# A four-layer graph network: first keys ahead of the branch, 125-row transfers on GpSimd, and the last block scanned in three parts

## The chip, the cores and the metric

The kernel runs on 1 core of one Trainium2 chip. The metric is the device time of one execution in microseconds (us). Engines: PE (TensorE) multiplies matrices, DVE (VectorE) works on vectors, ACT (ScalarE) evaluates functions, POOL (GpSimd) issues the indirect gathers and scatters here, SP (SyncE) issues most plain transfers.

## What is computed

There are N = 6250 nodes with D = 16 features and E = 200000 edges, sorted by their target `dst`. Each layer reads the source node's row for every edge, makes a message, combines the messages of each target, adds the node's own row and normalizes:

```
L0: m = tanh(x[src] * edge_weight);  x = layernorm(x + segment_sum(m, dst))
L1: attention over the edges (messages and weights from 16 edge features,
    softmax over each target's edges);  x = layernorm(x + ...)
L2: m = x[src] * edge_weight1;  x = layernorm(x + segment_max(m, dst) @ W.T + b)
L3: twice  h = relu(((1+eps)*h + segment_sum(h[src], dst)) @ wa + ba) @ wb + bb
    x = layernorm(x + log_softmax(h))
```

## The kernel before

**Layout.** Nodes lie on P = 125 partitions, NJ = 50 to each; edges on the same 125 partitions, J = 1600 consecutive ones to each. "Column" means one edge of each partition.

**Start.** SP loads dst, src and x. ACT's first instruction (`arrived`, L218) reads one element of src; behind it ACT's queue issues three copies from DRAM to DRAM (L220): `ew_d` and `ew1_d` (781 KB each) and `ef_d` (the edge features, 12.5 MB). DVE counts partitions whose dst isn't sorted (L225 to L230); every engine loads that number and branches (L231, L232): in the true branch `sort_edges` runs; with these inputs it is not taken. Behind the branch the keys of block 0 are made (`keys_made`, `keys_turned`, `keys_kept`, L246 to L280): DVE arithmetic on src, one transpose on PE, kT stored to `key_d` in DRAM (L274).

**edge_scan (L465)** runs four times: for L0, L2 and the two convolutions of L3 (l3a, l3b). The 1600 columns go in NB = 8 blocks of JB = 200. Of each block, the first NPE = 120 columns are fetched by PE: a batch of BC = 12 columns loads its keys (L456, SP, 367 KB, two batches ahead), DVE compares them with four node groups (`one_hot`, L462), and three `select`s of 4 columns each multiply one-hot matrices with the node table in SBUF (L491, 48 matmuls), after which DVE masks and reduces (L495, L500) into `xb`. The other 80 columns of the block are fetched by POOL, one indirect gather per column (L532, L97), of GP = 125 rows. Once a block is complete, DVE (and in L0 ACT) makes the message (`message`, L890/L891 in L0, L1292 in L2, nothing in L3), and 16 `tensor_tensor_scan`s, one for each feature, run along its 200 columns, beginning from the block before (L508 to L522). For blocks 0 to 6 this happens between the selects of the next block, two scans after each select; for block 7 it happens after the last select (L554 to L558). The running values are stored to `rows` in DRAM, and a short chain through PE carries totals between partitions (L560 to L584). The order of instructions in edge_scan is that of the program (`manual_schedule`).

**Side jobs.** In L0 the selects are numbered 0 to 239, and `prelude` (L893) hangs work onto them: keys of later blocks, the search for each node's last edge (`ends_*`), with 51 indirect run loads of 128 rows on POOL (`ends_gather`, L406), the chunk tables of L1, with 50 indirect scatters of 128 rows on POOL (`chunks_put`, L744), and the splitting of ef_d into `edges_d` (`edge_rows`). The edge weights `ew` of L0 are loaded on SP ahead of the scan (L887).

**at_nodes (L587)** follows each scan: 50 indirect gathers of 128 rows (`an_y`) fetch each node's last running value, in chunks `CHUNKS = ((0, 40), (40, 50))`; then `finish` makes the new node rows, stores them to the next table in DRAM (`into_table`) and splits them for PE. Its instructions are ordered by the scheduler, by estimates of cost.

**L1** runs 220 steps and then gathers its results, 50 indirect gathers of 128 rows into `r`, in groups of GN = 5 with 3 buffers; each group takes a Ln and an Exp on ACT, which load their function tables, and products and sums on DVE (L1224 to L1243).

Of the kernel before, what the change touches and what calls it, by code (L numbers as in the profile page):

```python
# [20 lines left out]
P = 125  # L21
# [20 lines left out]
CHUNKS = ((0, 40), (40, NJ))  # L42
# [5 lines left out]
def tile_gnn_resnorm(ctx: ExitStack, tc: tile.TileContext, a: dict, out: bass.AP):  # L48
# [166 lines left out]
    arrived = consts.tile([1, 1], F32, name="arrived")  # L215
    with tc.manual_schedule():

        nc.scalar.copy(arrived, src[:1, :1])  # L218
        for to, of in given[2:]:
            nc.scalar.dma_start(to.rearrange("(p j) f -> p (j f)", p=80),  # L220
                                of.rearrange("(p j) f -> p (j f)", p=80))
    with tc.tile_pool(name="sort", bufs=1) as sp, tc.tile_pool(name="sortp", bufs=1, space=PSUM) as pp:
        back = sp.tile([P, J], F32, name="backwards")
        worst = sp.tile([P, 1], F32, name="worst")
        nc.vector.tensor_tensor(back, dst[:, 1:J + 1], dst[:, :J], op=OP.is_lt)  # L225
        nc.vector.tensor_reduce(worst, back, AX.X, OP.max)
        n_ps = pp.tile([1, 1], F32, name="n_ps")
        nc.tensor.matmul(n_ps, worst, ones, start=True, stop=True)
        n_back = sp.tile([1, 1], I32, name="n_back")
        nc.vector.tensor_copy(n_back, n_ps)  # L230
        unordered = nc.values_load(n_back, min_val=0, max_val=P)  # L231
        with tc.If(unordered > 0):  # L232
            sort_edges(sp, pp, dst)
            nc.sync.dma_start(src, src_d.rearrange("(p j) o -> p (j o)", j=J))
            load_dst(dst, dst_d.rearrange("e o -> (e o)"))

# [42 lines left out]
    with tc.tile_pool(name="keys0p", bufs=1, space=PSUM) as pp:  # L279
        keys_kept(kp, 0, keys_turned(lambda r, c: pp.tile([128, 512], F32, name="scratch")[:r, :c], keys_made(kp, 0)))  # L280
# [74 lines left out]
    def ends_begin(sp):  # L355
        e = Ends()
        e.runs = sp.tile([P, NR + 1], F32, name="runs")
        nc.vector.tensor_copy(e.runs[:, :NR], dst[:, 1:J + 1].rearrange("p (r k) -> p r k", k=RUN)[:, :, RUN - 1])
        nc.vector.tensor_copy(e.runs[:, NR:], rank[:P])
        edge = sp.tile([P, 2], F32, name="dst_edge")  # L360
        nc.vector.tensor_copy(edge[:, 0:1], dst[:, :1])
        nc.vector.tensor_scalar(edge[:, 1:2], rank[:P], float(P - 1), BIG, op0=OP.is_equal, op1=OP.mult)
        nc.vector.tensor_add(edge[:, 1:2], edge[:, 1:2], e.runs[:, NR - 1:NR])

        e.from_ = sp.tile([P, 2, NJ1], F32, name="from_edge")
        nc.vector.tensor_tensor(e.from_, edge.unsqueeze(2).to_broadcast([P, 2, NJ1]),
                                io[:P, :NJ1].unsqueeze(1).to_broadcast([P, 2, NJ1]), op=OP.subtract)
        nc.vector.tensor_scalar(e.from_, e.from_, 1.0, None, op0=OP.add)
        e.run = sp.tile([P, NJ1], F32, name="run")
        e.run_i = sp.tile([128, NJ1], I32, name="run_i")  # L370
        nc.vector.memset(e.run_i[96:], 0)
        e.inside, e.row_ps = {}, {}
        return e
# [18 lines left out]
    def ends_runs(sp, e, j0):  # L392

        n = min(NS, NJ1 - j0)
        here = slice(j0, j0 + n)
        row_of = sp.tile([P, NS, NR + 1], F32, name="row_of")
        nc.vector.tensor_copy(row_of[:, :n], e.row_ps.pop(j0)[:, :n])
        less = sp.tile([P, NS, NR], F32, name="less")
        nc.vector.tensor_tensor(less[:, :n], row_of[:, :n, :NR], nodes[:, here].unsqueeze(2).to_broadcast([P, n, NR]),
                                op=OP.is_le)  # L400
        nc.vector.tensor_reduce(e.run[:, here], less[:, :n], AX.X, OP.add)
        nc.vector.scalar_tensor_tensor(e.run[:, here], row_of[:, :n, NR], float(NR), e.run[:, here], op0=OP.mult, op1=OP.add)
        nc.vector.tensor_scalar(e.run[:, here], e.run[:, here], float(E // RUN - 1), None, op0=OP.min)
        nc.vector.tensor_copy(e.run_i[:P, here], e.run[:, here])

    def ends_gather(sp, e):  # L406
        e.in_run = sp.tile([128, NJ1, RUN], I32, name="in_run")
        for j in range(NJ1):
            gather(e.in_run[:, j, :], runs_d, e.run_i[:, j:j + 1])

    def ends_upto(sp, e, j0):
        here = slice(j0, j0 + 17)
        less = sp.tile([P, 17, RUN], BF16, name="less_in")
        nc.vector.tensor_tensor(less, e.in_run[:P, here], nodes[:, here].unsqueeze(2).to_broadcast([P, 17, RUN]),
# [39 lines left out]
    def load_keys(ep, k, bufs=2):  # L454
        keys = ep.tile([P, BW], U16, name="keys", bufs=bufs)
        nc.sync.dma_start(keys, key_d[k * BC * P:k * BC * P + BW].partition_broadcast(P))  # L456
        return keys

# [6 lines left out]
    def edge_scan(tag, table, parts, F, message, pen, tmp, beside=None, first=None):  # L465
# [10 lines left out]
        with tc.tile_pool(name=f"es_{tag}", bufs=3) as ep, \  # L476
# [4 lines left out]
            NBT = NPE // BC  # L481
            batches = [(b, c) for b in range(NB) for c in range(NBT)]
# [19 lines left out]
            def scans(xb, b, prev):  # L502
# [3 lines left out]
                if prev is not None:  # L506
                    last = ep.tile([P, F], F32, name="last", bufs=2)
                    nc.vector.tensor_copy(last, prev[:, JB - 1, :])  # L508

                def one(f):  # L510
                    if is_max:
                        init = -BIG if last is None else last[:, f:f + 1]
                        nc.vector.tensor_tensor_scan(sc[:, :, f], pen[:, b * JB:(b + 1) * JB], xb[:, :, f],
                                                     init, op0=OP.add, op1=OP.max)
                    else:
                        init = 0.0 if last is None else last[:, f:f + 1]
                        nc.vector.tensor_tensor_scan(sc[:, :, f], keep[:, b * JB:(b + 1) * JB], xb[:, :, f],  # L517
                                                     init, op0=OP.mult, op1=OP.add)

                pieces = [lambda f=f: one(f) for f in range(F)]  # L520
                pieces.append(lambda: store(nc.sync, rows_v[:, b * JB:(b + 1) * JB, :], sc))
                return sc, pieces  # L522

            keys = [load_keys(ep, k) for k in range(0 if first is None else 1, 2)]
            ohs = one_hot(ep, keys.pop(0)) if first is None else first
            prev, todo, waiting = None, [], []
            for k, (b, c) in enumerate(batches):
# [10 lines left out]
                if c == 2 and waiting:  # L538
                    xw, bw = waiting.pop(0)
                    message(xw, bw)  # L540
                    prev, todo = scans(xw, bw, prev)
# [12 lines left out]
            for xw, bw in waiting:  # L554
                message(xw, bw)
                prev, todo = scans(xw, bw, prev)
                while todo:
                    todo.pop(0)()  # L558
# [150 lines left out]
    def chunks_set(tmp, num, stop, off_ps, all_ps):  # L709
# [16 lines left out]
        rows_all = tmp.tile([128, NJ, 4], F32, name="ck_rows")  # L726
        nc.vector.memset(rows_all[96:], 0.0)
        rows = rows_all[:P]
# [7 lines left out]
        at = tmp.tile([128, NJ], I32, name="ck_at")  # L736
        nc.vector.memset(at[96:], 128 * Q)
        nc.vector.tensor_copy(at[:P], first)
# [3 lines left out]
        return rows_all, at  # L742

    def chunks_put(rows_all, at):  # L744
        for j in range(NJ):
            nc.gpsimd.indirect_dma_start(
                out=chunk_d[j % NC], out_offset=bass.IndirectOffsetOnAxis(ap=at[:, j:j + 1], axis=0),
                in_=rows_all[:, j, :], in_offset=None, bounds_check=128 * Q - 1, oob_is_err=False)
# [138 lines left out]
    nc.sync.dma_start(ew, ew_d.rearrange("(p j) o -> p (j o)", j=J))  # L887

    def tanh_message(xb, b):
        nc.vector.tensor_mul(xb, xb, ew[:, b * JB:(b + 1) * JB].unsqueeze(2).to_broadcast([P, JB, D]))  # L890
        nc.scalar.activation(xb, xb, AF.Tanh)  # L891

    def prelude(kp):  # L893
# [65 lines left out]
        at(10, lambda: put(r=edge_rows_begin(now["rp"])))  # L959
        for i in range(J // WE):  # L960
            for step in range(4):
                at(16 + 3 * i + step, lambda i=i, step=step: edge_rows(now["r"], i * WE, step))
# [6 lines left out]
    rows, carry = edge_scan("l0", a["x"], parts, D, tanh_message, None, lp0, prelude(kp))  # L969
# [170 lines left out]
    first = one_hot(fp, load_keys(fp, 0, 1), 1)  # L1140
# [4 lines left out]
    with tc.tile_pool(name="l1t", bufs=1) as lp, tc.tile_pool(name="l1tp", bufs=1, space=PSUM) as pp:  # L1145
# [78 lines left out]
        for j0, j1 in CHUNKS:  # L1224
            n = j1 - j0
            y = lp.tile([P, n, D], F32, name=f"y1_{j0}")
            for j in range(j0, j1, GN):
                r = lp.tile([128, GN, RW], F32, name="r", bufs=3)
                for i in range(GN):
                    gather(r[:, i, :], rows1, idx_row_all[:, j + i:j + i + 1])  # L1230
                v = r[:P, :, :2 * DD].rearrange("p j (i k o) -> p j i k o", k=2, o=D)
# [3 lines left out]
                for i in range(GN):  # L1235
                    nc.vector.tensor_mul(A[:, i], A[:, i], L[:, i])
                    nc.vector.tensor_reduce(y[:, j - j0 + i, :], A[:, i].rearrange("p i o -> p o i"), AX.X, OP.add)
            nc.vector.tensor_mul(y, y, own[:, j0:j1].unsqueeze(2).to_broadcast([P, n, D]))
# [46 lines left out]
    with tc.tile_pool(name="l2", bufs=1) as lp:  # L1285
# [5 lines left out]
        def scaled_message(xb, b):  # L1291
            nc.vector.tensor_mul(xb, xb, ew1[:, b * JB:(b + 1) * JB].unsqueeze(2).to_broadcast([P, JB, D]))  # L1292

        rows, carry = edge_scan("l2", t2, parts, D, scaled_message, pen, lp, first=first)
        with tc.tile_pool(name="l2p", bufs=2, space=PSUM) as pp:
# [9 lines left out]
            at_nodes(lp, rows, carry, D, True, finish)  # L1305


    def gin(tag, table, parts, xt, F, ws, lp, then):
# [3 lines left out]
        rows, carried = edge_scan(tag, table, parts, F, lambda xb, b: None, None, lp, first=first)  # L1312
        with tc.tile_pool(name=f"{tag}p", bufs=2, space=PSUM) as pp:
# [21 lines left out]
            at_nodes(lp, rows, carried, F, False, finish)  # L1335
# [75 lines left out]
```

## Time and profile before

| what | us |
|---|---|
| median of 4 runs (7629.24 to 7634.75) | 7631.42 |
| the profiled execution | 7627.16 |
| its span, first to last instruction | 7625.4 |
| start, to the first matmul of L0 | 75.5 |
| L0 scan, POOL's first to last gather | 60.1 to 1220.2 |
| L0 running values done | 1238.4 |
| first gather of L1's steps' table | 1322.7 |
| L1's last step stored; end of its result gathers | 4217.9; 4297.8 |
| L2 gathers of xb | 4323.0 to 5333.1 |
| l3a gathers of xb | 5437.7 to 6432.0 |
| l3b gathers of xb | 6529.4 to 7522.0 |
| last store of out | 7622.4 |

| engine | busy us | share of the span |
|---|---|---|
| PE | 6790.1 | 89% |
| DVE | 6752.1 | 89% |
| POOL | 5864.3 | 77% |
| ACT | 1904.3 | 25% |

How to read it: the times of one profiled execution are counted from its first instruction; 1.8 us of the execution lie outside the span. A POOL row is the time in which POOL issues a gather, not that of the data's way. "idle before <- X" names what an engine waited for just before an instruction; "issue" is idle time without a recorded cause. L numbers are lines of the kernel before. In a row, `125x3200` is partitions x elements, and x16 stands for 16 instructions shown as one.

### The profile page before, as it was taken

Reading aid. Unit: us, or ns where it says so; the run is one execution under the profiler, and the core shown is the slowest. Engines: PE = TensorE matmul, PEld = TensorE weight load, DVE = VectorE, ACT = ScalarE, POOL = GpSimd, SP = SyncE. Lnnn points to the kernel's source line nnn. Section 1 sums busy time; section 2 is a strip of 40 time slices with the busy share of each in tenths; the row PEclk is TensorE's granted clock in tenths of the full one; section 3 lists DMA queues with packets and bytes.
Section 4 is the critical chain, followed back from the end, with each engine's and each line's share of the span. In section 5 each row is a group of like instructions: output and inputs, shape, how many; then the busy total and the mean of one; then the engine's idle time right before and its main releaser. Section 6 shows DMA issues by size and latency. Waiting matters only on the chain. (4 is left out here: it accounts for less than half of the span.)

```text
span 7625.4 us, 133196 instructions
## 1 busy us (share of the span) xinstructions
PE 6790.1 (89%) x55586; PEld 5218.0 (68%) x55586; DVE 6752.1 (89%) x7804; ACT 1904.3 (25%) x3200; POOL 5864.3 (77%) x4906
## 2 busy tenths in 40 slices
PE   5889894999999999999999499998599997899995
PEld 5888894444444444444444399998599996899994
DVE  6999995999999999999999789997589886688985
ACT  0122110555555555555555300000000000000000
POOL 5787886777777777777777588887688887788886
PEclk9999997999999999999999799999799998899997
DMA  4444542222222222222222422222122222122221
GB/s 129 94 113 100 124 94 76 48 53 50 53 50 52 53 50 53 50 53 52 51 53 48 134 45 45 56 51 40 36 46 54 47 54 45 30 53 47 55 45 32
DMA packets 288129, 460.34 MB, mean 60 GB/s; under 512 B 134733, under 2 KB 188133, under 8 KB 283216
## 3 DMA queue, kind: packets, MB, share of 16 engines
q1 hardware_dynamic: 121136, 331.29, 12.9%
q0 software_dynamic: 166032, 105.92, 12.8%
q10 hardware_dynamic: 336, 14.40, 0.6%
q8 instruction: 441, 7.23, 0.4%
q14 instruction: 184, 1.51, 0.1%
HBM read 256.64 MB, written 206.15 MB: 61 GB/s over the span
## 5 line engine op out<-in xcount | busy, mean ns | idle before, releaser
L491 PE MATMUL all_ps<-parts,oh 125*128 125x208 bf16 (+1 forms) x46080 | 4004.4, 251 | 205.1 <-DVE kept L495 77.4
L491 PEld LDWEIGHTS <-oh 125*128 125x128 bf16 x46080 | 3985.7, 98 | 223.8 <-issue 99.0
L97 POOL DMA_INDIRECT hg<-table_x,g x1760 | 2061.6, 1171 | 544.3 <-issue 540.6
L97 POOL DMA_INDIRECT xb<-table_x,src x1280 | 1614.7, 1262 | 434.8 <-issue 413.0
L1077 PE MATMUL la<-e,ident 128*128 128x512 f32 x3520 | 1560.3, 596 | 4.5 <-DVE e L1064 3.8
L500 DVE TENSOR_REDUCE xb<-kept 125x64 f32<-125x832 f32 x960 | 1508.2, 1571 | 33.1
L495 DVE TENSOR_TENSOR kept<-all_ps,place 125x832 f32<-125x832 f32 x960 | 974.6, 1015 | 346.7 <-PE all_ps L491 337.9
L1077 PEld LDWEIGHTS la<-e,ident 128*128 128x128 f32 x3520 | 652.2, 190 | 743.6 <-issue 737.2
L97 POOL DMA_INDIRECT xb<-in_x,src x640 | 835.9, 1306 | 251.0 <-issue 193.3
L1029 DVE TENSOR_TENSOR e<-mm,hg 128x1024 f32<-128x1024 f32 x880 | 1013.3, 1208 | 2.5 <-DMA hg<-table_x,g 2.2
L97 POOL DMA_INDIRECT xb<-table_l3b,src x640 | 797.7, 1246 | 211.6 <-issue 210.4
L1024 PE MATMUL mm<-w_h,eT 98*128 98x512 bf16 x1760 | 667.7, 379 | 237.7 <-DVE e L1029 168.2
L462 DVE TENSOR_SCALAR oh<-keys,mykey 125x1504 bf16<-125x1504 uint16 x1272 | 795.2, 685 | 73.0 <-DMA keys<-key_d 72.9
L1041 ACT ACTIVATE e<-e,epen 128x256 f32<-128x256 f32 x1760 | 797.7, 501 | 112.8 <-DVE e L1029 110.8
L1057 ACT ACTIVATE e<-e 128x1024 f32<-128x1024 f32 x440 | 465.1, 1057 | 1001.8 <-DVE e L1055 984.5
L1025 PE MATMUL mm<-w_l,eT 98*128 98x512 bf16 x1760 | 669.0, 380 | 0.0
L1025 PEld LDWEIGHTS <-eT 98*128 98x128 bf16 x1760 | 169.7, 96 | 636.9 <-issue 532.5
L1055 DVE TENSOR_TENSOR e<-e,st 128x1024 f32<-128x1024 f32 x440 | 519.5, 1222 | 7.6
L1064 DVE TENSOR_TENSOR e<-e 128x1024 f32<-128x1024 f32 x440 | 515.7, 1210 | 0.0
L1024 PEld LDWEIGHTS <-eT 98*128 98x128 bf16 x1760 | 170.8, 97 | 238.2 <-issue 56.5
L449 ACT ACTIVATE ln_s<-ln_s,eps_t 125x40 f32<-125x40 f32 (+1 forms) x8 | 2.4, 314 | 1181.5 <-DVE ln_s L448 1181.5
L97 POOL DMA_INDIRECT g<-edges_d,eidx x220 | 208.5, 948 | 91.9 <-PE la L1078 64.0
(366 smaller groups left out, 3390.2 us busy)
## 6 DMA issues: line engine op xcount, KB each, us to landing
keys<-key_d SPq DMA_DIRECT2D x318, 367.2 KB
rows_l<-st SPq DMA_DIRECT2D x220, 384.0 KB
edges_d<-er_t SPq DMA_DIRECT2D x64, 546.9 KB
hg<-table_x,g POOLq DMA_INDIRECT x1760, 2.6
rows_l<-sc SPq DMA_DIRECT2D x16, 1400.0 KB
xb<-table_x,src POOLq DMA_INDIRECT x1280, 2.7
ef_d<-in_edge_attr ACTq DMA_DIRECT2D x1, 12500.0 KB
er_ef<-ef_d SPq DMA_DIRECT2D x64, 175.0 KB
```

Of the source, the lines that this page charges most:

```text
L97: nc.gpsimd.indirect_dma_start(out=dst_ap, out_offset=None, in_=table, in_offset=bass.IndirectOffsetOnAxis(ap=idx, axis=0))
L462: nc.vector.tensor_scalar(oh[:, g, :], keys, mykey[:, g:g + 1], None, op0=OP.is_equal)
L491: nc.tensor.matmul(o, oh[:, g, (c + i) * P:(c + i) * P + 128], parts[:, q, a0:a0 + n, :].rearrange("p a f -> p (a f)"), start=(g == 0 and ...
L495: nc.vector.tensor_tensor(kept.rearrange("p (h i) a f -> p h (i a) f", i=2), all_ps[:P, :, :2 * W].rearrange("p h (i f) -> p h i f", f=F), ...
L500: nc.vector.tensor_reduce(xb[:, j:j + SG, :], kept.rearrange("p i a f -> p i f a"), AX.X, OP.add)
L1024: nc.tensor.matmul(ps[:, i, :], eT[:, s + i, :], w_h, start=True, stop=False)
L1025: nc.tensor.matmul(ps[:, i, :], eT[:, s + i, :], w_l, start=False, stop=True)
L1029: nc.vector.tensor_tensor(e[:, s:s + 2, :].rearrange("p s (i x) -> p (s i) x", x=2 * D), ps.rearrange("p s (i x) -> p (s i) x", x=2 * D), ...
L1041: nc.scalar.activation(part(e, 0)[:, k], part(e, 0)[:, k], AF.Identity, bias=epen[:, t, k:k + 1])
L1055: nc.vector.tensor_tensor(sc, sc, top.rearrange("p (i o) -> p i o", o=D).unsqueeze(1).to_broadcast([128, 4, D, D]), op=OP.subtract)
L1064: nc.vector.tensor_tensor(part(e, 1)[:, s:s + 4], part(e, 1)[:, s:s + 4], part(e, 0)[:, s:s + 4], op=OP.mult)
L1077: nc.tensor.matmul(ps, ident, e[:, s, :], start=(s == 0), stop=False)
```

## The change

Six edits, made together. (1) Counting stays first, but block 0's keys are made and the first two key batches are loaded before the branch; `arrived` reads the first key batch, so ACT's three copies are issued behind its landing; the copies are written with 1600 rows for 80. The true branch makes the keys again. (2) The load of `ew` becomes job 20 of the prelude, split in 112 and 13 partitions; `edge_rows_begin` goes from job 10 to 14 and the edge rows' jobs from 16 + 3i to 19 + 3i. (3) Run loads and chunk scatters use tiles of 125 rows, and three memsets of the spare rows go. (4) The last block of each scan is scanned in three parts: columns 0 to 71 between the last 12 selects, 72 to 119 after the last select, 120 to 199 when the gathers have landed. (5) CHUNKS becomes ((0, 35), (35, 50)), and at_nodes of L2, l3a and l3b takes the order of the program. (6) L1's result groups end in 3 and 2 instead of 5, with 4 buffers.

```diff
-CHUNKS = ((0, 40), (40, NJ))
+CHUNKS = ((0, 35), (35, NJ))
...
-        nc.scalar.copy(arrived, src[:1, :1])
-        for to, of in given[2:]:
-            nc.scalar.dma_start(to.rearrange("(p j) f -> p (j f)", p=80),
-                                of.rearrange("(p j) f -> p (j f)", p=80))
...
+    def keys_first(first):
+
+        with tc.tile_pool(name="keys0p", bufs=1, space=PSUM) as pp:
+            keys_kept(kp, 0, keys_turned(lambda r, c: pp.tile([128, 512], F32, name="scratch")[:r, :c], keys_made(kp, 0)))
+        return [load_keys(kp, k, to) for k, to in enumerate(first)]
...
+        unordered = nc.values_load(n_back, min_val=0, max_val=P)
+        keys0 = keys_first([None, None])
+        arrived = consts.tile([1, 1], F32, name="arrived")
+        with tc.manual_schedule():
+
+            nc.scalar.copy(arrived, keys0[0][:1, :1])
+            for to, of in given[2:]:
+                nc.scalar.dma_start(to.rearrange("(p j) f -> p (j f)", p=1600),
+                                    of.rearrange("(p j) f -> p (j f)", p=1600))
+        with tc.If(unordered > 0):
+            sort_edges(sp, pp, dst)
+            nc.sync.dma_start(src, src_d.rearrange("(p j) o -> p (j o)", j=J))
+            load_dst(dst, dst_d.rearrange("e o -> (e o)"))
+            keys_first(keys0)
...
-        e.run_i = sp.tile([128, NJ1], I32, name="run_i")
-        nc.vector.memset(e.run_i[96:], 0)
+        e.run_i = sp.tile([P, NJ1], I32, name="run_i")
...
-        e.in_run = sp.tile([128, NJ1, RUN], I32, name="in_run")
+        e.in_run = sp.tile([P, NJ1, RUN], I32, name="in_run")
...
+            CE = NBT - 4
...
+                if b == NB - 1 and c == CE:
+
+                    assert not todo
+                    message(xb, b, 0, CE * BC)
+                    sc, last = scans(b, prev)
+                    todo = pieces(xb, b, sc, last, 0, CE * BC)
...
-            for xw, bw in waiting:
-                message(xw, bw)
-                prev, todo = scans(xw, bw, prev)
-                while todo:
-                    todo.pop(0)()
+            for lo, hi in ((CE * BC, NPE), (NPE, JB)):
+                message(xb, b, lo, hi)
+                for do in pieces(xb, b, sc, last, lo, hi):
+                    do()
+            keep_rows(sc, b)
+            prev = sc
...
-        rows_all = tmp.tile([128, NJ, 4], F32, name="ck_rows")
-        nc.vector.memset(rows_all[96:], 0.0)
-        rows = rows_all[:P]
+        rows = tmp.tile([P, NJ, 4], F32, name="ck_rows")
...
-        at = tmp.tile([128, NJ], I32, name="ck_at")
-        nc.vector.memset(at[96:], 128 * Q)
-        nc.vector.tensor_copy(at[:P], first)
+        at = tmp.tile([P, NJ], I32, name="ck_at")
+        nc.vector.tensor_copy(at, first)
...
-    nc.sync.dma_start(ew, ew_d.rearrange("(p j) o -> p (j o)", j=J))
...
-        at(10, lambda: put(r=edge_rows_begin(now["rp"])))
+        at(20, lambda: store(nc.sync, ew, ew_d.rearrange("(p j) o -> p (j o)", j=J)))
+        at(14, lambda: put(r=edge_rows_begin(now["rp"])))
...
-            for j in range(j0, j1, GN):
-                r = lp.tile([128, GN, RW], F32, name="r", bufs=3)
-                for i in range(GN):
+            j = j0
+            for m in [GN] * (n // GN - 1) + [GN - 2, 2]:
+                r = lp.tile([128, GN, RW], F32, name="r", bufs=4)
+                for i in range(m):
...
-            at_nodes(lp, rows, carry, D, True, finish)
+            with tc.manual_schedule():
+                at_nodes(lp, rows, carry, D, True, finish)
```

`pieces(xb, b, sc, last, lo, hi)` makes the 16 scans of columns lo to hi of a block, which begin from the column before lo; `load_keys` takes a tile to load into. Messages take lo and hi as well.

## Prediction

> **What bounds the kernel now.** I read the page's 40 slices first, then the waits and the timeline of the first 80 us, then POOL's instructions tile by tile, then the timeline at the end of each scan.
>
> ```profile
> PE   5889894999999999999999499998599997899995
> DVE  6999995999999999999999789997589886688985
> POOL 5787886777777777777777588887688887788886
> L97 POOL DMA_INDIRECT xb<-in_x,src x640 | 835.9, 1306 | 251.0 <-issue 193.3
> ```
>
> A slice is 191 us. PE, DVE and POOL are all nearly full in layer 0 (slices 2 to 6), so who ends last has to be read at its end. The gather row tells it for POOL: 640 gathers of 1.306 us busy and 193.3 of issue (0.30 each) make 1029 us of the 1160 between its first gather (60.05) and its last (1220.22). The 51 run loads (49.7 + 15.5 idle) and the 50 chunk scatters (50.2 + 15.2) make 131 more: 1160, so POOL never rests in layer 0. A microsecond that POOL starts later, or an instruction that costs it more, arrives at the end of layer 0 whole.
>
> Timeline at that end (start, duration, engine, line, what was waited for):
>
> ```profile
> 1220.22 1.21 POOL L97 DMA_INDIRECT xb<-in_x,src  x1 [0.30 <-issue]
> 1223.42 3.49 DVE L890 TENSOR_TENSOR xb<-xb,ew 125x3200 f32<-125x3200 f32 x1 [4.27 <-DMA xb<-in_x,src]
> 1226.95 2.87 ACT L891 ACTIVATE xb<-xb 125x3200 f32<-125x3200 f32 x1 [98.06 <-DVE xb L890]
> 1229.85 8.52 DVE L517 TENSOR_TENSOR_SCAN sc<-keep,last,xb 125x200 f32<-125x200 f32 x16 [2.85 <-ACT xb L891]
> ```
>
> DVE had ended its selects and waited 4.27 us for the last gather; then message, tanh and 16 scans stand alone for 15.0 us (1223.4 to 1238.4).
>
> Waits of the first 80 us, then its timeline:
>
> ```profile
> POOL xb L97 <- DMA key_d<-kT: 56.2, 1, 56.2
> DVE oh L462 <- DMA keys<-key_d: 45.0, 1, 45.0
> ```
> ```profile
> 11.18 0.19 ACT L218 CAST arrived<-src 1x1 f32<-1x1 int32 x1 [9.14 <-DMA src<-in_src]
> 12.45 0.60 ACTq L220 DMA_DIRECT2D ef_d<-in_edge_attr  x1
> 22.64 0.22 DVE L249 CAST key_df<-src 125x120 f32<-125x120 int32 x1 [10.09 <-DVEq L232]
> ...
> 59.03 0.30 SPq L887 DMA_DIRECT2D ew<-ew_d  x1
> 59.45 0.32 SPq L274 DMA_DIRECT2D key_d<-kT  x1
> 60.05 1.39 POOL L97 DMA_INDIRECT xb<-in_x,src  x1 [56.16 <-DMA key_d<-kT]
> ...
> 74.44 4.27 DVE L462 TENSOR_SCALAR oh<-keys,mykey 125x1504 bf16<-125x1504 uint16 x6 [45.01 <-DMA keys<-key_d]
> ```
>
> POOL's first gather needs x and src only, both there by 11.2, yet starts at 60.05, just when SP issues again (59.03). The page names the kT store as releaser, but that is issued at 59.45 and is no input of a gather. In the built program SP, on the side of the branch that is taken (no sorting), waits for every DMA lane in turn, the three copies' included, and the first work of each engine behind the branch waits for SP's last count. The 12.5 MB copy ef_d, issued at 12.45, is what SP waits for until 59. **The start is bound by the copies, through the branch.**
>
> **1. Start.** In the changed program that join is still there, in the same order of lanes: POOL's first gather, DVE's first one-hot and PE's first weights wait for the count that SP gives after ef_d has landed. But the copies now wait for the first key batch. The chain: n_back at 12.45; the key operations, 22.64 to 29.42 now, take 6.8 (to 19.3); kT's store 0.3 and a landing of 2.5, taken from the 32.5 KB table store of 1320.21, after which POOL goes on at 1322.70 (22.1); the key load 6.3 (68.12 to 74.44; 28.4). ACT's copy thus moves from 11.18 to 28.4, +17.2, and the copies with it: SP's join comes at 76.2, POOL's first gather at 77.3. The bounds: 14 if the key load takes 4, as a short one, 23 if the store takes the 8.7 that SP's own key load waited (59.45 to 68.12, beside the ew load). DVE has its keys by then, so the first one-hot stands at about 77 instead of 74.4 and PE loses 2.5. The whole gain of keys made early goes into this wait; POOL loses **17**. The copies' new shape (1600 rows for 80) changes nothing: both build to the same transfers.
>
> **2. Rows of 125.** POOL's instructions by tile (minimum/median/maximum ns):
>
> ```profile
> L97 POOL DMA_INDIRECT xb<-in_x,src x640: 1206/1212/4523, 60.1 to 1220.2; - x160
> L97 POOL DMA_INDIRECT in_run<-runs_d,run_i x51: 941/945/1577, 315.8 to 379.8; - x51
> L746 POOL DMA_INDIRECT chunk_d<-ck_rows,ck_at x50: 972/974/1335, 639.6 to 703.8; - x50
> ```
>
> xb has 125 rows, in_run and the chunks 128, and within one layer, beside the same DVE work, the 125-row gather costs POOL more. Every other 128-row gather here (an_y, g, r, hg's fastest) has a minimum of 0.94, and hg reads the very table that layer 2's 125-row xb reads at 1.205. So I take the rows to be the reason. Means: 51 x (1.306 - 0.974) = 16.9, 50 x (1.306 - 1.004) = 15.1: **+32** on POOL. Bounds: 3/128 less of 99.9 us busy, -2.3, if time goes by rows; +47, if all go like the slower xb gathers of 1.45. The value is the means', since these operations would stand between xb gathers of that mean. Three DVE memsets that go are below 0.5.
>
> [...]
>
> **3. Does POOL's lateness end last?** 17 + 32 = 49: POOL's last gather at 1269. DVE had little to give: block 4's message stands 19 us behind POOL's last gather of that block (833.4 and 852.6), block 6's 28 (1094.0 and 1122.5). DVE, itself 2.5 late, will wait some 30 us in block 4 and end its selects near 1255, including part 1's scans; part 2 then fits ahead of 1272. So POOL stays last and the 49 arrive.
>
> **4. Last block in three parts.** Columns 0-72 go between the last selects, 72-120 after them; both need no gather. Behind the last landing stand 80 of 200 columns: message 3.49 x 0.4 = 1.4, tanh 2.87 x 0.4 = 1.2, scans 16 x 0.30 (0.533 each in the row above, less 120 columns at about 1.95 ns, from the scans of 125 columns, 0.41, and 239, 0.625) = 4.8: 7.5 for 15.0, **-7.5**. Layer 2 has no tanh: **-5.7**. Both convolutions of layer 3: 8.53 - 4.8, **-3.7** each. Cover: DVE waits for the last gathers 20.6 in layer 2 and 8.5 in l3a, part 2's scans take 16 x 0.24 = 3.8; if that cover were gone, up to 4.5 (part 1) comes back in each.
>
> **5. Node chunks 35 + 15, chunk 0 finished first.** Layer 2: from the last ends landed (5419.25) to the table store (5431.84) are 12.6 us, in which chunk 0's layernorm and its table store (3.7 us on SP) run between chunk 1's steps. In the new order chunk 0, landed 6.3 earlier, is done by about 5416; 15 nodes alone take about 8: **-4.5**. l3a: 10.3 (6514.48 to 6524.81) becomes 7.5: **-2.8**. l3b: chunk 0, with its three function tables, ends about 2 after chunk 1 lands (7604.5), then 14.5 for 15 nodes: 7621 for 7622: **-1**. Layer 0: its last 3.7 grow by half as many nodes again, about **+1**.
>
> **6. Layer 1's end.** POOL stalls on the third r buffer (0.6 + 2.2 + 3.8 + 2.7 around 4241 to 4259) shrink with a fourth; the last group is 2 nodes for 5. From the last gather (4296.83) to the table store (4319.97) are 23.1, now with chunk 0's layernorm in between; two short groups with four table loads of 1.28 (7.7), their products (2) and 15 nodes' layernorm (5) make about 16. With some 4 of stall: **-10** (-4 to -14; each further group costs ACT 2.6 of table loads, which 96 us cover).
>
> The edge weights' load and the edge rows' jobs move by a few selects; the weights are first read at 267, the rows needed at 1246: nothing.
>
> **Sum:** +17.2 + 32 - 7.5 + 1 - 10 - 5.7 - 4.5 - 3.7 - 2.8 - 3.7 - 1 = **+11**. The profiled execution took 7627.2, so it would take 7638; the median of the four runs is 7631.4, 4.3 above it, and the same 11 make **7642**.
>
> **Rivals.**
> *125 rows cost POOL no more* than 128; xb's 1.21 is due to something else, such as its index list. For: no row shows these two operations at 125. Against: all 128-row tables agree. Then 11 - 34 = -23: 7608.
> *The start really moves ahead*: the gathers don't wait for ef_d and start near 30. For: keys ready at 28.4. Against: the lanes that SP waits for. 11 - 17 - 29 = -35: 7596.
> *Slower: the two sets go like the slow xb gathers.* Run loads have rows of 160 bytes, scatters write to DRAM; at 1.45 they cost 47 instead of 32: 7657. It decides from 1.35 a gather, 0.05 above my value, since 101 x 0.05 takes the sum past +15.
> *Slower: the tails don't shrink*, as part 1 delays the last selects and short chunks pay for their fixed steps: half of the 39 saved goes, 7661.
>
> **How the numbers follow.** What a measurement tells from no change is about 0.2%, 15 us. My sum 0.58 (own range 7630 to 7655; 0.41 within 15, 0.17 above), equal rows 0.17 (0.15 faster, 0.02 same), early start 0.05 (faster), slow sets 0.14 and tails 0.06 (slower). Faster 0.20, same 0.43, slower 0.37. The range reaches from the equal rows to the slow sets and full tails with their spread: 7602 to 7664.
>
> **What would show it.** POOL's first gather near 77 and PE's first matmul near 78; in_run and the scatters at 1.2 to 1.3; POOL's last gather of layer 0 near 1269, with a DVE wait of some 30 us for block 4's gathers; scans of 80 columns in 4.8 behind each last landing; layer 2's table store about 8 after its last ends. I am wrong if the gather starts near 30, if the 125-row sets stay at 0.95, or if DVE, not POOL, ends layer 0.

## The result and the profile after

| | median us | runs | ratio to before, 95% interval |
|---|---|---|---|
| before | 7631.0 | 58 | |
| changed | 7645.9 | 38 | 1.0019 (1.0015 to 1.0024) |

The change costs 14.9 us (11 to 18 by the interval): clear of zero, and just below the 15 us that the prediction called a difference. The forecast was +11. The profiled execution of the changed kernel took 7648.1 with a span of 7646.3, 20.9 more than the span of before; of these two single executions the first lies 2 above its median and the second 4 below, so stages compared below add up to 21, not to 15.

The page's slices and its gather row, changed kernel:

```profile
PE   5898795899999999999999499999499997799995
DVE  6999895899999999999999788999489887688985
POOL 5888887777777777777777488888688887788886
L97 POOL DMA_INDIRECT xb<-in_x,src x640 | 834.7, 1304 | 266.2 <-issue 193.9
```

Nothing there tells the two kernels apart, and the gathers of layer 0 cost what they did (1304 ns for 1306). What moved is in the stages. The start, changed kernel (waits of the first 85 us, then timeline):

```profile
POOL xb L97 <- SPq L289: 71.5, 1, 71.5
DVE oh L469 <- SPq L289: 55.2, 1, 55.2
```
```profile
19.27 0.37 SPq L252 DMA_DIRECT2D key_d<-kT  x1
21.33 0.65 SPq L262 DMA_DIRECT2D keys<-key_d  x2
27.17 0.19 ACT L285 CAST arrived<-keys 1x1 f32<-1x1 uint16 x1 [25.13 <-SPq L289]
...
28.45 0.60 ACTq L287 DMA_DIRECT2D ef_d<-in_edge_attr  x1
74.41 4.62 DVE L469 TENSOR_SCALAR oh<-keys,mykey 125x1504 bf16<-125x1504 uint16 x8 [55.17 <-SPq L289]
...
75.37 1.56 POOL L97 DMA_INDIRECT xb<-in_x,src  x1 [71.47 <-SPq L289]
```

The keys are in SBUF at 27 and lie there until 74: now the trace itself names SP's side of the branch (L289) as the releaser of POOL and DVE. POOL starts at 75.4 instead of 60.1, PE at 75.1 instead of 75.5: before, too, the first one-hot came at 74.4, when the keys had landed.

POOL's instructions by tile, changed kernel:

```profile
L97 POOL DMA_INDIRECT xb<-in_x,src x640: 1205/1212/4535, 75.4 to 1262.2; - x160
L97 POOL DMA_INDIRECT in_run<-runs_d,run_i x51: 1206/1212/1604, 331.8 to 409.8; - x51
L769 POOL DMA_INDIRECT chunk_d<-ck_rows,ck_at x50: 1186/1190/3079, 670.2 to 747.7; - x50
```

At 125 rows the run loads take exactly the xb gathers' 1212 ns, the scatters 1190. DVE's wait in block 4, and the end of layer 0:

```profile
876.47 3.53 DVE L912 TENSOR_TENSOR xb<-xb,ew 125x3200 f32<-125x3200 f32 x1 [24.18 <-DMA xb<-in_x,src]
```
```profile
1262.15 1.21 POOL L97 DMA_INDIRECT xb<-in_x,src  x1 [0.30 <-issue]
1265.15 1.49 DVE L912 TENSOR_TENSOR xb<-xb,ew 125x1280 f32<-125x1280 f32 x1 [18.00 <-DMA xb<-in_x,src]
1266.68 1.27 ACT L914 ACTIVATE xb<-xb 125x1280 f32<-125x1280 f32 x1 [23.06 <-DVE xb L912]
1267.98 4.53 DVE L533 TENSOR_TENSOR_SCAN sc<-keep,sc,xb 125x80 f32<-125x80 f32 x16 [1.34 <-ACT xb L914]
```

POOL ends block 4 40 us later than before and the layer 42 us later. That costs DVE 24 us in block 4 and 18 at the end; before, DVE waited for gathers only at the end, for 4.3. Behind the last landing stand 7.4 us instead of 15.0.

By stages, in us, from POOL's rows and the tables' stores in both profiled executions (L1's first gather is that of its edge features, `g`):

| stage | forecast | measured |
|---|---|---|
| POOL's first gather of L0 | +17 | +15.3 |
| to POOL's last gather of L0 | +32 | +26.6 |
| L0's tail, to L1's first gather | -7.5 | -8.3 |
| L0's nodes, to the table's store | +1 | +0.6 |
| L1's steps | 0 | +0.6 |
| L1's end, first r gather to L2's first gather | -10 | +4.5 |
| L2's 640 gathers | 0 | +3.4 |
| L2's tail, to l3a's first gather | -10.2 | -11.5 |
| l3a's gathers | 0 | -0.7 |
| l3a's tail, to l3b's first gather | -6.5 | -5.4 |
| l3b's gathers | 0 | +0.9 |
| l3b's tail, to the last store | -4.7 | -4.9 |
| sum | +11 | +21.0 |

### The profile page after: what moved, and what is told of

The parts are those of the page before. It is cut to its first block, busy times and chain, and to the rows that moved or that the text cites. A ratio compares the mean times of both kernels' runs of the same rounds, so it can differ in the third digit from the quotient of the medians.

```text
span 7646.3 us, 133337 instructions
## 1 busy us (share of the span) xinstructions
PE 6795.8 (89%) x55586; PEld 5219.9 (68%) x55586; DVE 6776.5 (89%) x7933; ACT 1915.4 (25%) x3214; POOL 5898.9 (77%) x4906
## 3 DMA queue, kind: packets, MB, share of 16 engines
q1 hardware_dynamic: 121160, 331.29, 12.9%
## 5 line engine op out<-in xcount | busy, mean ns | idle before, releaser
L97 POOL DMA_INDIRECT xb<-in_x,src x640 | 834.7, 1304 | 266.2 <-issue 193.9
L1053 DVE TENSOR_TENSOR e<-mm,hg 128x1024 f32<-128x1024 f32 x880 | 1013.0, 1208 | 11.3 <-DMA hg<-table_x,g 10.5
```

What stands on the lines that cost most here:

```text
L97: nc.gpsimd.indirect_dma_start(out=dst_ap, out_offset=None, in_=table, in_offset=bass.IndirectOffsetOnAxis(ap=idx, axis=0))
L1053: nc.vector.tensor_tensor(e[:, s:s + 2, :].rearrange("p s (i x) -> p (s i) x", x=2 * D), ps.rearrange("p s (i x) -> p (s i) x", x=2 * D), ...
```

## The experiments

The theory: the time is POOL's in layer 0 (a later start through the branch, dearer transfers), partly paid back by the tails. The rivals: the rows cost nothing by themselves; DVE or PE would have ended layer 0 anyway; edit 6 or the early keys have a price that the forecast lacks. Times are compared with the runs of before on the same chip; the changed kernel, which was not run beside them, stands at +14.9. The intervals reach 7 to 11 us to each side, so small differences from the changed kernel are read from the stages of the profiles.

**1. The rows alone, on the kernel before.**

```diff
-        e.run_i = sp.tile([128, NJ1], I32, name="run_i")
-        nc.vector.memset(e.run_i[96:], 0)
+        e.run_i = sp.tile([P, NJ1], I32, name="run_i")
...
-        at = tmp.tile([128, NJ], I32, name="ck_at")
+        at = tmp.tile([P, NJ], I32, name="ck_at")
```

> The kernel before with edit 3 alone: run loads and chunk scatters of 125 rows for 128. Theory (125 rows cost POOL more): each of the 51 run loads and 50 scatters about 0.27 and 0.22 us longer at the median, their two sets some 14 us longer each, POOL's last gather of layer 0 28 us later, and 28 us on the whole: 7659. Rival (rows cost nothing by themselves, the changed kernel's rows were longer for another reason): medians stay at 0.945 and 0.974 and the time at 7631.

Measured 7652.0, ratio 1.0029 (1.0017 to 1.0040), +21. The two sets take 14.6 and 12.7 us longer, and their medians are 1.212 and 1.190. POOL's last gather of layer 0 comes 22.0 later: other blocks took back 5 of the 27.

**2. The changed kernel with 128 rows again** (the same lines, back).

> The changed kernel with run loads and chunk scatters of 128 rows again. Theory: 28 us less than the changed kernel, 7618, so 13 faster than before; POOL's last gather of layer 0 near 1234 instead of 1262. Rival (DVE or PE, not POOL, would end layer 0 without the long rows): less than half of the 28 comes, 7632 or more.

Measured 7622.4, ratio 0.9991 (0.9982 to 1.0000): 23.6 less than the changed kernel. POOL's last gather is at 1237.3. The rival, less than half of the 28, falls. The rows alone turn this change from a small gain, if it is one (its interval ends at 1.0000), into a small loss.

**3. The copies behind the branch.**

```diff
-            nc.scalar.copy(arrived, keys0[0][:1, :1])
...
         with tc.If(unordered > 0):
...
             keys_first(keys0)
+    nc.scalar.copy(arrived, keys0[0][:1, :1])
...
```

> The changed kernel with the three copies issued behind the branch instead of ahead of it; all else as changed. Theory (the branch makes every engine wait for the copies): the first gather at 31 to 36 instead of 75.4, PE's first matmul at about the same time, layer 0 some 40 us earlier, 7606. Rival (the copies then run beside the first selects and gathers and take back what was won): first gather early, but POOL's and PE's first block longer by 20 us or more, 7625 or more.

Measured 7629.4, ratio 0.9997 (0.9988 to 1.0006): 16.6 less than the changed kernel, not 40. The first gather is at 32.7 and the first matmul at 32.5, as the theory said; but block 0 takes POOL 153 us instead of 125, and from PE's first matmul to block 0's message there are 227 us instead of 192. POOL's busy time by stretch (columns: stretch, length, busy and instructions, granted clock, share of the DMA engines, GB/s), this kernel and then the changed one with the copies out of the way:

```profile
33.00:78.00 45.00, 19.60 (x15) 0.85 0.97 315
78.00:186.00 108.00, 82.39 (x65) 0.92 0.29 66
```
```profile
75.00:120.00 45.00, 36.35 (x28) 1.00 0.24 58
```

While the copies run, the DMA engines are 97% busy and POOL gets 15 gathers through where it gets 28 otherwise. So the rival was right: freed of the branch, POOL issues its last gather of block 0 at 185.7, no earlier than the kernel before (184.1). Of the 43 us by which the gathers start earlier than in the changed kernel, the copies take 28 back; the 15 that are left are what edit 1 had lost against before.

**4. Layer 1's end as before, on the changed kernel.**

```diff
...
-            for m in [GN] * (n // GN - 1) + [GN - 2, 2]:
-                r = lp.tile([128, GN, RW], F32, name="r", bufs=4)
+            for m in [GN] * (n // GN):
+                r = lp.tile([128, GN, RW], F32, name="r", bufs=3)
...
-    first = one_hot(fp, load_keys(fp, 0), 1)
+    first = one_hot(fp, load_keys(fp, 0, None, 1), 1)
```

> The changed kernel with layer 1's end as before: groups of 5, three r buffers, one buffer for the first keys. Theory (edit 6 lost time there, since the first keys' load and the ew1 load came to stand just ahead of the r gathers): 50 r gathers in 73 us for 82, layer 2 starting 4 to 5 us earlier, 7641. Rival (edit 6 gained the 10 us that were forecast, and the loss lies elsewhere): 10 us more, 7656.

Measured 7652.0, ratio 1.0028 (1.0016 to 1.0039): 6 more, not 5 less. The times alone would not settle it, but the stage does: the r gathers take 86.7 us for 81.6, and layer 2 starts 8.0 later than in the changed kernel. Edit 6 is a gain and the loss in this stage lies elsewhere, as the rival said without saying where. SP's timeline shows what this kernel shares with the changed one (changed kernel, then before):

```profile
4256.83 0.27 SPq L262 DMA_DIRECT2D keys<-key_d  x1
4257.38 0.48 SPq L1315 DMA_DIRECT2D ew<-ew_d  x1
4257.58 0.95 POOL L97 DMA_INDIRECT fx<-rows_l,fix_row  x1 [32.53 <-PE own_ps L1244]
```
```profile
1320.91 0.26 SPq L456 DMA_DIRECT2D keys<-key_d  x1
...
4230.16 0.27 SPq L1289 DMA_DIRECT2D ew<-ew_d  x1
```

Layer 2's first keys, loaded at the begin of layer 1's steps before (1320.91), are now loaded at their end, and the load of edge_weight1 comes 1.4 us ahead of the first r gather instead of 6.1 behind it. ACT then waits 12.9 us for the first group's r (changed kernel), where its longest such wait was 3.4 (the last fence, before):

```profile
ACT L1258 <- DMA r<-rows_l,idx_row: 16.5, 3, 12.9
ACT now L1201 <- DMA r<-rows_l,idx_row: 14.0, 1, 14.0
DVE tT L1203 <- ACT now L1201: 12.5, 2, 12.2
```
```profile
ACT L1233 <- DMA r<-rows_l,idx_row: 16.7, 9, 3.4
```

In the changed kernel DVE's carry chain, queued on ACT, waits with it.

**5. Room for the first keys.** Block 0's key tiles (edit 1) lie in a pool that stays open through layer 1. Here they get their own, closed after layer 0's scan. Layer 2's first keys go back from two buffers to one; the second had come with the new `load_keys`, and the list of edits does not name it.

```diff
+    k0 = ctx.enter_context(ExitStack())
+    kq = k0.enter_context(tc.tile_pool(name="keys0k", bufs=1))
...
-        return [load_keys(kp, k, to) for k, to in enumerate(first)]
+        return [load_keys(kq, k, to) for k, to in enumerate(first)]
...
+    k0.close()
...
-    first = one_hot(fp, load_keys(fp, 0), 1)
+    first = one_hot(fp, load_keys(fp, 0, None, 1), 1)
```

> The changed kernel with block 0's two key tiles in a room of their own, given back after layer 0's scan, and one buffer for layer 2's first keys as before; in the built program that load then stands at the begin of layer 1's steps again, not behind them. Theory (the two key tiles, kept through layer 1, pushed the load and the one-hots of layer 2's first keys to the end of layer 1, and there they delay the r gathers): 50 r gathers in 68 to 72 us for 81.7, layer 2 starting some 12 us earlier, 7634. Rival (the stalls of the r gathers come from the groups and ACT's order): 7646.

Measured 7629.5, ratio 1.0005 (0.9996 to 1.0014): +3.6, 11.3 less than the changed kernel. Layer 2's first keys are loaded at the begin of layer 1's steps again (1355.2), and edge_weight1 6.1 us behind the first r gather. The r gathers take 68.9 us for 81.6, layer 2 starts 12.9 earlier. From the first r gather to layer 2's first are 90.7 us, 8.3 less than before: edit 6 itself is worth 8 of the 10 that were forecast. Experiment 4 had the single buffer too and kept the late load, so the buffer alone does not do it: the key tiles' room is what was missing. Which of the two moved loads, or ACT's order that moved with them, holds the r gathers was not tried apart.

**6. The last block in one part, on the changed kernel.**

```diff
-                if b == NB - 1 and c == CE:
...
-            for lo, hi in ((CE * BC, NPE), (NPE, JB)):
+            sc, last = scans(b, prev)
+            for lo, hi in ((0, JB),):
```

> The changed kernel with the last block scanned in one part behind the gathers, as before; messages too. Theory: the four tails grow by 8, 6, 4 and 4 us: 22 more, 7668. Rival (the parts ahead of the gathers cost the last selects as much as they save): within 5 us of the changed kernel, 7646.

Measured 7654.1, ratio 1.0037 (1.0023 to 1.0051): 13 more than the changed kernel, between theory and rival. The tails grow by 7.7, 5.8, 2.6 and 2.6, 19 in all; but the gathers of layer 0 end 3.4 earlier, those of layer 2 take 4.1 less, and those of l3a and l3b 1.1 less each. The parts cost POOL something, most in the two layers that have a message (the last section shows how).

**7. Chunks and order as before** (`CHUNKS = ((0, 40), (40, NJ))`, no `manual_schedule` around at_nodes).

> The changed kernel with node chunks of 40 and 10 and at_nodes ordered by the scheduler again. Theory: layer 2's tail grows by 5, l3a's by 2 to 3, l3b's by 1, layer 0's shrinks by 1: 7 to 8 more, 7653. Rival (the order gains nothing, all of the tails' gain is the scan's parts): 7646.

Measured 7652.8, ratio 1.0036 (1.0022 to 1.0050): 12 more. Layer 2's tail grows by 5.3, l3a's by 1.7, l3b's by 0.7, near the prediction's 4.5, 2.8 and 1; the span is 10 above the changed kernel's, 2 of it in l3b's gathers.

**8. All gathers of 128 rows, on the kernel before.**

```diff
-GP = 125
+GP = 128
```

> The kernel before with the 80 gathers of each block taking 128 rows for 125, nothing else. Theory (125 rows cost POOL 0.27 us more than 128, whatever the table): the median gather 0.945 for 1.212; POOL no longer ends the scans, DVE's last waits (20.6, 8.5, about 8 and 4.3 us) go, 7590. Rival (xb's 1.21 has another reason than its rows): median 1.21 and 7631.

Measured 7577.2, ratio 0.9936 (0.9922 to 0.9950): 49 less, from one number.

```profile
L97 POOL DMA_INDIRECT xb<-in_x,src x640: 940/944/3573, 59.9 to 1138.0; - x160
L97 POOL DMA_INDIRECT xb<-table_l3b,src x640: 938/944/1307, 6485.0 to 7399.5; - x160
```

The same gathers from the same tables take 0.944 for 1.212. The edit changes nothing but the number of rows. POOL no longer ends the scans: in l3b its last gather stands 91 us ahead of the first end gather (7490.3), where 19 were before.

**9. POOL's time by the number of rows.** One more gather ahead of every eighth, with ROWS[b] rows in block b.

```diff
-GP = 125
+GP = 128
+ROWS = (127, 126, 125, 124, 120, 112, 96, 64)
...
+                        if j % 8 == 0:
+                            gather(xb_all[:ROWS[b], j, :], table, src_all[:ROWS[b], b * JB + j:b * JB + j + 1])
```

> The kernel before with gathers of 128 rows, and in each block, ahead of every eighth gather, one more of the same column with fewer rows: 127, 126, 125, 124, 120, 112, 96 and 64 in blocks 0 to 7. It measures POOL's time against the number of rows; the extra 320 gathers make it longer. Theory A (a number that 16 doesn't divide costs more): 127, 126, 125, 124 and 120 take about 1.2, 112, 96 and 64 take 0.95 or less. [...] Theory C (time goes by rows, 128 is a special case): falling evenly below 1.21 from 127 to 64.

Its 320 extra gathers make it 8165 (one execution). A gather of 127 rows and its neighbours of 128 (block 0 of l3b):

```profile
6958.92 0.94 POOL L98 DMA_INDIRECT xb<-table_l3b,src  x1 [0.31 <-issue]
6960.17 2.56 POOL L98 DMA_INDIRECT xb<-table_l3b,src  x1 [0.30 <-issue]
6965.92 0.95 POOL L98 DMA_INDIRECT xb<-table_l3b,src  x1 [3.19 <-DMA xb<-table_l3b,src]
```

Medians in l3b, of ten gathers of each size and of their neighbours of 128; "divisor" is the largest number up to 16 that divides the rows:

| rows | 128 | 127 | 126 | 125 | 124 | 120 | 112 | 96 | 64 |
|---|---|---|---|---|---|---|---|---|---|
| divisor | 16 | 1 | 14 | 5 | 4 | 15 | 16 | 16 | 16 |
| POOL us | 0.945 | 2.561 | 0.994 | 1.206 | 1.304 | 0.991 | 0.942 | 0.926 | 0.915 |

Theory A falls: 126 and 120 rows, which 16 doesn't divide, take 0.994 and 0.991, not 1.2. So does theory C: 124 rows take more than 125, and 127 the most of all. In this one execution the nine times go by the divisor instead: 2.561 us at 1, 1.304 at 4, 1.206 at 5, 0.994 and 0.991 at 14 and 15, 0.915 to 0.945 at 16. It is POOL's issuing that takes longer, by 0.26 us at 125 rows and 1.6 at 127 against 128. Why the divisor counts was not shown.

**10. Three repairs together on the changed kernel** (2, 3 and 5).

> The changed kernel with three repairs together: run loads and scatters of 128 rows, the copies behind the branch, block 0's keys in a room given back after layer 0. Theory (three separate losses): their single gains add up, 24 + 16 + 11 = 51 below the changed kernel, 7595; less in layer 0 if DVE ends it once POOL is 40 us earlier. Rival (POOL's gain in layer 0 is cut off by DVE and PE at about 1219): 7605 to 7615.

Measured 7591.2, ratio 0.9951 (0.9938 to 0.9965): 37 less than before, 52 less than the changed kernel; the single gains were 24, 17 and 11. They add up.

**11. And the columns shared out anew.**

```diff
-GP = 125
+GP = 128
...
-NPE = 120
+NPE = 108
...
-            CE = NBT - 4
+            CE = 6
```

> The kernel of those three repairs, with gathers of 128 rows and 92 of each block's 200 columns on POOL for 80, 108 on PE for 120; the last block's first part still 72 columns. Theory (a 128-row gather has a period of 1.25 us): 92 x 8 x 1.25 = 920 us of POOL in a scan of layer 3, PE 991 x 108/120 = 892, so a scan of 920 to 930 for 992; four scans save 60 to 70 each, with the start and the tails 7340 to 7400. Rival (gathers and selects share something, DMA engines or SBUF, and the period grows with the load): 960 or more a scan, 7480 or more.

Measured 7344.1, ratio 0.9627 (0.9614 to 0.9640): 284 us less than before. A scan of l3b takes POOL 929 us for 991, as worked out: a period of 1.26 holds for 92 gathers a block beside the selects.

## Why the prediction was right

The mechanism was right: POOL ends layer 0, it starts later through the branch and pays for 125 rows, and the tails pay most of it back. The closeness of +11 to +14.9 is in part luck. Layer 1's end came out 14.5 us dearer than forecast and layer 2's gathers 3.4, while rows, start and tails came out 5, 2 and 1 cheaper; the two profiled executions are 21 apart, the medians 15.

1. **Start**, +17: measured +15.3. The chain was right; the key load took 5.8 and ACT's copy came at 27.2 instead of 28.4. (By its own terms the lower bound is 14.9, not 14.) PE, forecast at 78, started at 75.1 and lost nothing. The rival of an early start fell, and so did its price: it was put at 29 us under before, but once the gathers do start at 32.7 (experiment 3) POOL ends block 0 no earlier than before.
2. **Rows**, +32: the sets measured +28 in the changed kernel (their gaps between blocks 81.1 and 80.7 for 66.8 and 67.0), +27 in experiment 1, and 25 at POOL's last gather in experiment 2. The term was mis-sized: the mean of the xb gathers (1.306) holds their own long ones, and the sets' means came to 1.255 and 1.274. The rows' medians, 51 x 0.267 + 50 x 0.238 = 25.5, would have been nearer. The rivals of equal rows and of rows at 1.45 both fell.
3. **POOL last, DVE waiting**: 24.2 us in block 4 for "some 30", part 2 done ahead of the last landing with 18 to spare.
4. **Three parts**: layer 0's tail of -8.3, and 4.53 us of scans for 4.8. Not foreseen: some 3 us that the parts cost POOL in layers 0 and 2 each (last section).
5. **Chunks**: l3a and l3b within 1.2 of the forecast, scan and chunks together; layer 2 1.3 better.
6. **Layer 1's end**, -10, measured +4.5: this step failed. The fourth buffer and the short groups are worth 8 (experiment 5), but edit 1's two key tiles keep their room through layer 1 and push layer 2's first keys behind the steps. I had followed the early keys through time and queues, not through SBUF. Why the r gathers take 81.6 us with the loads at that place and 68.9 without stays open.

## What to carry to other kernels

Let the partitions of an indirect transfer be a number that 16 divides, and pad to it: here gathers of 128, 112, 96 and 64 rows took POOL 0.915 to 0.945 us (experiment 9), 125 for 128 cost 0.27 us a gather, and 128 rows everywhere, with the columns shared out anew, are worth 3% (experiment 11 against 10). A tile made earlier lives longer, so look in the built program for loads that lost their room. Ask what is under way ahead of a branch: here POOL, DVE and PE waited behind it for a copy that none of them reads, until 75 us, and started at 32 to 33 with the copy issued behind it, though most of that gain went to the copy again.

## What the runs showed of the hardware

A gather that POOL begins while a DVE message runs ends, but for one, 1.08 to 1.10 us behind the message. Messages and the gathers beside them, kernel before and then the changed one:

```profile
562.34 3.48 DVE L890 TENSOR_TENSOR xb<-xb,ew 125x3200 f32<-125x3200 f32 x1
563.35 3.55 POOL L97 DMA_INDIRECT xb<-in_x,src  x1 [0.30 <-issue]
```
```profile
5310.10 1.34 DVE L1318 TENSOR_TENSOR xb<-xb,ew 125x1152 f32<-125x1152 f32 x1
5310.14 2.39 POOL L97 DMA_INDIRECT xb<-table_x,src  x1 [0.30 <-issue]
```

In the kernel before, 14 of the 14 gathers that begin within a message end 1.08 to 1.09 us after it, whatever their start; the changed kernel's shorter message holds its gather in the same way (5311.44 and 5312.53). In the changed kernel 17 of 18 end 1.08 to 1.10 us behind theirs; the other begins 0.01 us into its message (876.48) and takes 1.21. What makes a gather wait for a message was not shown. The gather at 5310.14, 2.39 us for 1.21, accounts for 1.2 of the 3 us that parts 1 and 2 cost POOL in the last block of layer 2. The other is a gather of 3.15 beside part 2's 16 scans:

```profile
5354.53 3.45 DVE L530 TENSOR_TENSOR_SCAN sc<-pen,sc,xb 125x48 f32<-125x48 f32 x16
5355.90 3.15 POOL L97 DMA_INDIRECT xb<-table_x,src  x1 [0.30 <-issue]
```

It ends 1.07 us behind the last scan (5359.04 and 5357.98), and so do the gathers beside part 2's scans in the three other scans of the changed kernel (1248.22 and 1247.15, 6463.74 and 6462.67, 7549.29 and 7548.22). So scans can hold a gather too, but not every one: layer 0's gather at 1244.13 took 1.21 beside the same scans. What decides it was not tried.
